# A graph network's edge kernel: the columns' list, the weights and the checks at other places, and two more groups by column copies

## The chip, the cores and the metric

The kernel runs on one core of a Trainium2 chip. The core has five engines, each with its own list of instructions that it works off in order: PE (matrix products; its weight loads are shown as a row of their own, PEld), DVE (vector operations), ACT (activation functions and copies), POOL (here: gathers of rows by index) and SP (which only issues transfers). PE writes to PSUM, a small memory that DVE and ACT read; everything else lies in SBUF, 128 partitions wide. Engines wait for one another through semaphores. Transfers from and to HBM are issued by SP, ACT or POOL and carried out by 16 DMA engines.

The metric is the device time of one launch in microseconds (us), the median of several executions. One further execution was profiled: its span runs from the first to the last instruction.

## The reference

One layer of message passing over 12,500 nodes with 64 features and 200,000 edges sorted by destination, then a residual and a normalisation:

```python
msg_in = concatenate([x[src], x[dst], edge_attr], axis=-1)     # 200000 x (64 + 64 + 32)
messages = relu(msg_in @ mW1 + mb1) @ mW2 + mb2                # hidden width 128, out 64
aggregated = segment_sum(messages, dst, 12500)
upd_in = concatenate([x, aggregated], axis=-1)
y = x + relu(upd_in @ uW1 + ub1) @ uW2 + ub2
out = (y - mean(y)) / sqrt(var(y) + 1e-5)                      # per node
```

All of it is in float32. The destinations are not uniform: low node numbers have more edges.

## The kernel before, in words

**Tables.** `x @ mW1[:64]` (for the source) and `x @ mW1[64:128] + mb1` (for the destination) are computed once per node. The first goes to a table `tab_a` in HBM, from which POOL gathers rows by source index; the second to `tab_b`, of which windows of 32 consecutive rows are read, because sorted edges have neighbouring destinations.

**Tiles and groups.** The edges form 1563 tiles of 128. Six tiles are a *group* `s` (261 groups, the steps of the main loop), twelve tiles a *super-group* `g`. For a group, `edge_part(s)` (line 401) multiplies, tile by tile, a stationary operand `l` (32 edge features and a 32-row selection of the destination, made by DVE in `select_rows`, L276) with `rhs` (edge weights and the window of `tab_b`) into the PSUM tile `pc` (L414). `node_part(s)` (422) adds the gathered rows by a product with the identity (L443) and notes the tile for DVE's relu (`positive`, L467). `collect(s)` (485) sums the hidden rows `h` by destination into PSUM (`sums`, L507) and counts them (`cnt`, L503).

**Copied groups.** For some groups, listed in `COPIED`, the last two of the six tiles are not gathered. Instead the 128 source columns of the transposed features (`xtop`, `xbot` in SBUF) are copied one by one into a tile `xc`, some by ACT (`singly`, L384) and some by DVE (`joined`, L392); each copy handles one column for two tiles, its address read from the list `col_a` by a register load (L360, one for eight copies). PE then multiplies `xc` with the first weights (L417). `PACE` holds pairs (first step, groups per step); `progress(s)` sums them, and a group is copied piece by piece so that it is ready three steps before its use. `col_a` is made in `columns_list()` (333): two loads from HBM into a tile of the pool tag `tb` (four buffers, shared with the chunks of the tables), then four DVE operations (L342).

**Updates.** Every few steps a block of up to 416 nodes is complete; `update`, `activated`, `residual`, `squares`, `statistics`, `deviation`, `norm` and `store` carry it through the second network to the output. The first update comes at step 46. For it the second layers are folded in advance in `weights()` (857): PE and DVE by turns (L860 to L873).

**Checks.** The kernel is written for destinations that fit its windows. `checks()` (875) tests that: the largest and the smallest offset in `drc` (two reductions over 1563 columns, L880 and L881), the order of the windows (L885), the size of the update blocks. The result is a flag, read at the very end (L1033); where it is set, a general loop follows that does not run here.

**Order of the work.** The order on each engine is written out by hand. Start-up (lines 741 to 827) makes `tab_a` in 13 chunks (`chunk_a`), each with copies by ACT and DVE into a `tb` buffer and a write by SP; between them stand loads, the first selections and the addresses of all windows (`offsets`). Then `columns_list()` is called, then the main loop (915). In a step `s` PE's order is: `node_part(s)`, `collect(s - 1)`, parts of updates, from step 11 on now and then a chunk of `tab_b`, `edge_part(s + 1)`, and what `rest(s)` (829) issues. `rest` loads in steps 1 to 7 what `drc` needs, issues at step 11 (`BS`) the loads of the second layers on ACT's queue and fills constants on DVE, and calls at step 13 `weights()` and `checks()`. Gathers on POOL are paced: most of them wait for a named matmul. After step 257 a tail written out by hand (992 to 1030) finishes the last groups and blocks.

## Time and profile before

| | us |
|---|---|
| median of 3 executions (lowest, highest) | 2132.93 (2130.94, 2138.86) |
| the profiled execution, its own time | 2131.12 |
| its span, first to last instruction | 2129.4 |
| busy PE / PEld | 1680.7 / 1272.8 |
| busy ACT | 1568.5 |
| busy POOL | 1250.2 |
| busy DVE | 1177.9 |

The mean granted clock of PE was 0.783 of full speed; it moves between 0.5 and 1 within the span. In the first 53 us the DMA engines are 80% busy, in the next 53 us 70%, later 20 to 30%. A row of the profile names the kernel's line, the engine, the operation, the tile written and those read, how often, the busy time and the mean length of one; behind the bar comes how long the engine was idle just before, and what ended that. "issue" means that nothing in the profile explains the wait.

### The profile page before, as it was taken

To read this page: it belongs to the slowest core of one execution; us is meant where nothing else is said; L and a number is where in the kernel's file an instruction comes from. 1 tells how busy PE (TensorE), PEld (TensorE's weight loads), DVE (VectorE), ACT (ScalarE), POOL (GpSimd) and SP (SyncE) were. 2 spreads that over 40 slices of the span, in tenths; PEclk is the share of its full clock that TensorE was granted. 3 is DMA by queue.
4 is the path that set the end of the run, shared out by engine and by line. 5 is a ranking of instruction groups with operands and counts; after the bars stand their busy time and mean duration, and the time that the engine had idled before them with its cause. 6 is when DMAs were issued, how large, how long until landed. Compare 5 with 4: busy or idle time off the path is not lost. (4 is left out here: it accounts for less than half of the span.)

```text
span 2129.4 us, 48279 instructions
## 1 busy us (share of the span) xinstructions
PE 1680.7 (79%) x10746; PEld 1272.8 (60%) x10746; DVE 1177.9 (55%) x8420; ACT 1568.5 (74%) x8066; POOL 1250.2 (59%) x1330
## 2 busy tenths in 40 slices
PE   3577877887787778777877887887888888888887
PEld 3465656665555556555555656665666666666666
DVE  5436565555555555565554555555555555555555
ACT  2296968759869687789686877777776868687773
POOL 6564665666666566665665555655566666666660
PEclk7677787787787777777887777877787788788889
DMA  8723333322222222223222322323232333333331
GB/s 204 192 77 92 89 95 89 96 85 73 80 75 79 75 75 82 76 79 84 77 82 78 89 80 81 89 83 92 85 85 81 92 87 92 88 93 88 90 88 53
DMA packets 207649, 190.05 MB, mean 89 GB/s; under 512 B 57814, under 2 KB 173998, under 8 KB 207358
## 3 DMA queue, kind: packets, MB, share of 16 engines
q1 hardware_dynamic: 163292, 100.05, 16.7%
q0 software_dynamic: 42272, 85.08, 14.5%
q10 hardware_dynamic: 1794, 1.80, 0.4%
q8 instruction: 90, 1.47, 0.3%
q14 instruction: 201, 1.64, 0.3%
HBM read 168.76 MB, written 18.02 MB: 88 GB/s over the span
## 5 line engine op out<-in xcount | busy, mean ns | idle before, releaser
L242 POOL DMA_INDIRECT xg<-tab_a,src_s x1273 | 1201.6, 944 | 807.5 <-issue 267.4
L384 ACT ACTIVATE xc<-xtop,xbot 128x1 f32 x7912 | 1499.0, 280 | 166.8 <-issue 136.7
L392 DVE TENSOR_TENSOR xc<-xtop,xbot 128x1 int32 x7576 | 634.0, 154 | 494.4 <-issue 479.0
L507 PE MATMUL sums<-band,h 128*128 128x96 f32 x3126 | 538.4, 326 | 155.4 <-issue 107.5
L507 PEld LDWEIGHTS sums<-band,h 128*128 128x128 f32 x3126 | 475.5, 232 | 185.3 <-issue 121.2
L443 PE MATMUL pc<-xg,band 128*128 128x256 f32 (+1 forms) x988 | 447.6, 582 | 27.8 <-issue 26.7
L414 PE MATMUL pc<-rhs,l 64*128 64x128 f32 x3126 | 370.6, 356 | 70.3 <-issue 60.6
L414 PEld LDWEIGHTS pc<-rhs,l 64*128 64x128 f32 x3126 | 293.3, 238 | 122.1 <-issue 94.2
L467 DVE TENSOR_SCALAR h<-pc 128x768 f32<-128x768 f32 x247 | 235.1, 952 | 175.7 <-remote 59.4
L443 PEld LDWEIGHTS pc<-xg,band 128*128 128x128 f32 x988 | 214.8, 240 | 141.1 <-issue 97.0
L276 DVE TENSOR_TENSOR l<-l,cps 128x768 f32<-128x768 int32 (+1 forms) x134 | 126.9, 947 | 132.7 <-PE pc L443 38.8
L503 PEld LDWEIGHTS <-one 128*1 128x1 bf16 x1563 | 57.0, 81 | 224.5 <-issue 219.9
L588 ACT ACTIVATE y<-cps 128x256 f32<-128x256 f32 (+1 forms) x36 | 13.7, 379 | 174.8 <-issue 106.2
L503 PE MATMUL cnt<-band,one 128*1 128x32 bf16 x1563 | 90.7, 180 | 55.3 <-issue 54.8
L571 ACT ACTIVATE hTu<-sums,ub_s 128x416 f32<-128x416 f32 (+1 forms) x36 | 21.6, 599 | 127.9 <-remote 47.4
L417 PE MATMUL pc<-band,xc 64*128 64x128 f32 x484 | 77.4, 313 | 8.5 <-issue 6.8
L679 PE MATMUL pb<-band,xtop 64*128 64x128 f32 x208 | 48.2, 396 | 44.8 <-DVE tb L687 29.4
L284 DVE TENSOR_TENSOR band<-cps,drc 128x384 f32<-128x384 f32 x131 | 71.5, 546 | 19.0 <-remote 16.1
L679 PEld LDWEIGHTS pb<-band,xtop 64*128 64x128 f32 x208 | 40.7, 286 | 53.0 <-DVE tb L687 31.2
L417 PEld LDWEIGHTS pc<-band,xc 64*128 64x128 f32 x484 | 63.9, 227 | 9.8 <-issue 9.7
L581 PE MATMUL cps<-u2c,hTu 128*128 128x64 f32 x284 | 54.0, 340 | 14.6 <-issue 14.0
L242 POOL DMA_INDIRECT xg<-in_x,src_s x48 | 47.6, 992 | 24.0 <-issue 12.8
(110 smaller groups left out, 646.1 us busy)
## 6 DMA issues: line engine op xcount, KB each, us to landing
l<-in_dst_row SPq DMA_DIRECT2D x262, 96.0 KB
l<-in_eT SPq DMA_DIRECT2D x262, 96.0 KB
xg<-tab_a,src_s POOLq DMA_INDIRECT x1273
rhs<-tab_b SPq DMA_DIRECT2D x361, 32.0 KB
tab_b<-tb SPq DMA_DIRECT2D x13, 512.0 KB
rhs<-tab_b SPq DMA_DIRECT2D x387, 16.0 KB
tab_a<-tb SPq DMA_DIRECT2D x12, 512.0 KB
out<-y SPq DMA_DIRECT2D x35, 128.0 KB
```

What stands on the lines that cost most here:

```text
L242: ins = nc.gpsimd.indirect_dma_start(out=a[:, i, :] if s < XG else a[:, i // 2, i % 2, :], out_offset=None, in_=A[:, :] if s >= XG else x[ ...
L276: nc.vector.tensor_tensor(l[r], l[r].bitcast(I32), node[r].unsqueeze(2).broadcast_to([r.stop - r.start, SUP // 2, P]), op=ALU.is_equal)
L284: nc.vector.tensor_tensor(s[:, :nt], slot.unsqueeze(1).broadcast_to([P, nt, WIN]), drc[:, g * SUP:g * SUP + nt].unsqueeze(2).broadcast_to( ...
L384: nc.scalar.activation(o[:, e:e + 1], top.bitcast(F32), AF.Identity, bias=bot.bitcast(F32))
L392: nc.vector.tensor_tensor(o[:, e:e + 1].bitcast(I32), top.bitcast(I32), bot.bitcast(I32), op=ALU.bitwise_or)
L414: done = nc.tensor.matmul(pc[:, b, k, :], L[g][q:q + 64, m, :], rhs[g % 2][q:q + 64, w, :], start=k == 0, stop=ends and not copied)
L417: done = nc.tensor.matmul(pc[:, b, k, :], xc[s][q:q + 64], w1a[q:q + 64], start=False, stop=ends)
L443: added = nc.tensor.matmul(pc[:, b, :m], ident, a[:, b, :m], start=False, stop=True)
L467: nc.vector.tensor_scalar(h, pc, 0.0, None, op0=ALU.max)
L503: nc.tensor.matmul(pn8[:, bass.ds(cs[i] - CBASE, 4 * WIN)].bitcast(F32), one, SB[g][:, k0 + i, :, 1], start=False, stop=ends and i == n - 1)
L507: made.append(nc.tensor.matmul(ps8[:, bass.ds(ws[i] - SBASE[u % 2], 4 * WIDE * WIN)].bitcast(F32), h[:, i % 2, i // 2, :], widened(g, k0 + i),
L679: nc.tensor.matmul(pb[:, h, i, :], (xbot if h else xtop)[64 * h:64 * h + 64, (c + HB * h + i) * P:(c + HB * h + i + 1) * P], w[64 * h:64 * ...
```

## The change

1. `columns_list()` is split. `columns_asked()` issues the two loads of the list in start-up behind the ninth chunk (k == 8) instead of after the last; `columns_list(cols)` makes `col_a` on DVE behind the twelfth chunk (k == 11).
2. The seven loads of the second layers, on ACT's queue, move from step 11 of the loop to start-up, one behind each of the chunks 2 to 8; the constants' fills on DVE move there too, behind chunk 1. `weights()` moves from step 13 to step 1.
3. `checks()` is cut in four. The part on windows and blocks, `nodes_checked()`, stays at step 13; the two large reductions, `largest()` and `smallest()`, and the flag, `flagged()`, go to the tail.
4. `PACE` changes: copies start at step 5 instead of 3, with 0.54 groups per step up to step 30, then 0.5, and from step 50 on 0.004 to 0.008 groups per step more than before. 123 groups instead of 121 are copied; the list of which ones shifts by a step over large stretches.

```diff
-PACE = ((3, 0.474), (50, 0.501), (130, 0.479), (170, 0.465), (261, 0))
+PACE = ((5, 0.54), (30, 0.5), (50, 0.505), (130, 0.487), (170, 0.473), (261, 0))
...
-        def columns_list():
+        def columns_asked():
...
+            return cols
+
+        def columns_list(cols):
+
+            for r in range(2):
+                n = min(P, NSUB - 1 - LEAD - r * P)
                 for b, base in enumerate((XBASE, YBASE)):
                     nc.vector.tensor_scalar(col_a[:n, r, :, b], cols[:n, r, b], 4.0, float(base), op0=ALU.mult, op1=ALU.add)
...
+        weight_loads = {2: (w2, mW2), 3: (u1a, uW1[D:2 * D, :]), 4: (b2c, mb2.rearrange("(f o) -> f o", o=1)),
+                        5: (uz[D:], uW1[0:D, :]), 6: (ux[ONE:ONE + 1], ub2.rearrange("(o f) -> o f", o=1)),
+                        7: (ub1_s, ub1.rearrange("(f o) -> f o", o=1)), 8: (u2, uW2)}
         for k, c in enumerate(range(0, NB, NCH)):
             copied = chunk_a(c)
...
+            if k == 1:
+                nc.vector.memset(uz[:D], 0.0)
...
+                nc.vector.tensor_copy(ux[D:], ident[D:, D:])
+            if k in weight_loads:
+                o, i = weight_loads[k]
+                nc.scalar.dma_start(o, i)
+            if k == 8:
+                cols = columns_asked()
+            if k == 11:
+                columns_list(cols)
...
-        columns_list()
         assert not first
...
             if s == BS:
                 nc.sync.dma_start(wa, wrow.rearrange("o (p c) -> (o p) c", c=NSUP))
                 nc.sync.dma_start(wb, wnext.rearrange("o (p c) -> (o p) c", c=NSUP))
-                nc.scalar.dma_start(w2, mW2)
...
-                nc.scalar.dma_start(u2, uW2)
+            elif s == 1:
+                weights()
             elif s == BS + 2:
-                weights()
-                checks()
+                nodes_checked()
...
+        def largest():
+
+            nc.vector.tensor_reduce(mm[:, 0:1], drc, AX.X, ALU.max)
+
+        def smallest():
+
+            nc.vector.tensor_reduce(mm[:, 1:2], drc[:, :NT - 1], AX.X, ALU.min)
+
+        def flagged():
+
+            r = E - (NT - 1) * P
+            nc.vector.tensor_tensor(mm[:r, 1:2], mm[:r, 1:2], drc[:r, NT - 1:], op=ALU.min)
+            nc.vector.tensor_scalar(mm[:, 0:1], mm[:, 0:1], float(WIN - 1), None, op0=ALU.is_gt)
+            nc.vector.tensor_scalar(mm[:, 1:2], mm[:, 1:2], 0.0, None, op0=ALU.is_lt)
+            nc.vector.tensor_reduce(mm[:, 3:4], mm[:, 0:3], AX.X, ALU.add)
+            pf = psum.tile([1, 1], F32, name="pf", tag="pc")
+            nc.tensor.matmul(pf, mm[:, 3:4], ones, start=True, stop=True)
             nc.vector.tensor_tensor(flag_i, pf, bad, op=ALU.add)
...
         close_sums(K - 2)
+        largest()
         residual(K - 3)
...
         norm(K - 3)
+        smallest()
         store(K - 3)
...
         update(K - 1)
+        flagged()
         activated(K - 1)
```

More of the change, by code (lines that the diff above doesn't have):

```diff
@@ L819, in gnn_kernel @@
                 counts(g)
+            if k == 1:
+                nc.vector.memset(uz[:D], 0.0)
+                nc.vector.memset(ux[:D], 0.0)
+                nc.vector.memset(eps, EPS)
+                nc.vector.memset(ones, 1.0)
+                nc.vector.tensor_copy(ux[D:], ident[D:, D:])
[6 more added lines that the diff above has]
+                columns_list(cols)
             if k > 3:
@@ L873, in weights, with nodes_checked @@
                 nc.vector.tensor_scalar(w, v, mean, None, op0=ALU.subtract)
-        def checks():
-            mm = work.tile([P, 4], F32, name="mm", bufs=1)
-            r = E - (NT - 1) * P
-            nc.vector.tensor_reduce(mm[:, 0:1], drc, AX.X, ALU.max)
-            nc.vector.tensor_reduce(mm[:, 1:2], drc[:, :NT - 1], AX.X, ALU.min)
-            nc.vector.tensor_tensor(mm[:r, 1:2], mm[:r, 1:2], drc[:r, NT - 1:], op=ALU.min)
+        mm = work.tile([P, 4], F32, name="mm", bufs=1)
+        bad = work.tile([1, 1], F32, name="bad", bufs=1)
+        def nodes_checked():
             back = work.tile([SUP, NSUP], F32, name="back", bufs=1)
@@ L887, in checks @@
             nc.vector.tensor_reduce(mm[:SUP, 2:3], back, AX.X, ALU.add)
-            nc.vector.tensor_scalar(mm[:, 0:1], mm[:, 0:1], float(WIN - 1), None, op0=ALU.is_gt)
-            nc.vector.tensor_scalar(mm[:, 1:2], mm[:, 1:2], 0.0, None, op0=ALU.is_lt)
-            nc.vector.tensor_reduce(mm[:, 3:4], mm[:, 0:3], AX.X, ALU.add)
-            pf = psum.tile([1, 1], F32, name="pf", tag="pc")
-            nc.tensor.matmul(pf, mm[:, 3:4], ones, start=True, stop=True)
             uf = work.tile([1, K + 1], F32, name="uf", bufs=1)
```

11 lines of the change are left out of this document (removed).

## The prediction

> **What bounds the kernel now.** I read the page first: busy times, the chain, the costliest groups.
>
> ```profile
> span 2129.4 us, 48279 instructions
> PE 1680.7 (79%) x10746; PEld 1272.8 (60%) x10746; DVE 1177.9 (55%) x8420; ACT 1568.5 (74%) x8066; POOL 1250.2 (59%) x1330
> ...
> L242 POOL DMA_INDIRECT xg<-tab_a,src_s x1273 | 1201.6, 944 | 807.5 <-issue 267.4 <-remote 193.4 <-PE pc L443 127.4
> L384 ACT ACTIVATE xc<-xtop,xbot 128x1 f32 x7912 | 1499.0, 280 | 166.8 <-issue 136.7
> L392 DVE TENSOR_TENSOR xc<-xtop,xbot 128x1 int32 x7576 | 634.0, 154 | 494.4 <-issue 479.0
> ...
> L417 PE MATMUL pc<-band,xc 64*128 64x128 f32 x484 | 77.4, 313 | 8.5 <-issue 6.8
> ```
>
> No engine is full. PE is the busiest, and the gathers on POOL are held back on purpose until chosen matmuls are done (their idle time ends at L443). ACT and DVE spend most of their time on column copies. So I asked for the waits of the whole run, and for the span of one line that runs in every step.
>
> ```profile
> PE sums L507 <- DVE h L467: 34.0, 20, 4.8
> ...
> DVE h L467 <- PE sums L507: 55.7, 29, 4.2
> ...
> PE sums L507 <- DVE xc L392: 12.5, 6, 3.4
> ```
>
> ```profile
> L507 PE MATMUL sums<-band,h x3126: 242/275/530, 78.0 to 2120.5; 128*128 128x96 f32 x196
> ```
>
> The loop runs from 78.0 to 2120.5 us, 261 steps, so 7.83 us a step. PE waits for DVE in it 20 + 6 times, 46.5 us in all; DVE waits for PE longer (55.7 us in one row alone). PE's order of work therefore sets the pace, and what stops PE early in the loop delays all that follows. The change is about such stops, so I then read step 13, where the weights are prepared and the checks made (rows of PE, then of DVE, in order of time: start, length, what, in brackets the idle time before).
>
> ```profile
> 183.40 0.49 PE L417 MATMUL pc<-band,xc 64*128 64x128 f32 x4
> 184.93 0.30 PE L860 MATMUL pw<-band,w 128*64 128x128 f32 x1 [1.04 <-DVE xc L392]
> 187.91 0.79 PE L864 MATMUL pw<-u1a,w2T 64*128 64x128 f32 x2 [2.69 <-DVE w2T L862]
> 189.09 0.58 PE L867 MATMUL pw<-u1a,b2c 64*1 64x128 f32 x2 [0.39 <-DVE w2u L865]
> 195.65 0.19 PE L892 MATMUL pf<-ones,mm 128*1 128x1 f32 x2 [5.97 <-DVE mm L890]
> 195.77 2.08 PE L443 MATMUL pc<-xg,band 128*128 128x256 f32 x4
> ```
>
> ```profile
> 187.58 0.28 DVE L862 COPY w2T<-pw 64x128 f32<-64x128 f32 x1 [1.53 <-remote]
> ...
> 191.12 1.77 DVE L880 TENSOR_REDUCE mm<-drc 128x1 f32<-128x1563 f32 x1
> ...
> 194.69 0.28 DVE L885 TENSOR_TENSOR back<-wb,wa 12x131 f32<-12x131 int32 x1
> ```
>
> From 183.89 to 195.77 PE does next to nothing: it goes back and forth with DVE over the weights, then waits 5.97 us for DVE's checks, because the small matmul L892 stands in PE's order ahead of the gathered rows' sum (L443).
>
> **The change, part by part.** All terms are against this execution's own time, 2131.1 us (span 2129.4); it stands 1.8 us under the median of the runs shown and near the lowest.
>
> Step 13 empties. The weights' three matmuls and the checks' matmul leave it; what stays (L885 and its followers, on DVE alone) has no PE instruction behind it. PE goes from L417 to L443: 195.77 - 183.89 = **-11.9 us**. Bounds: -11.9, and -5.9 if the next steps make half of it up (a rival below).
>
> The clock after it. These windows give busy time by engine, then the granted clock (PEclk).
>
> ```profile
> 190.00:196.00 6.00, 0.35 (x3) 0.32 (x4) 5.69 (x19) 6.00 (x34) 0.00 (x0) 0.50 0.04 12
> 196.00:201.00 5.00, 5.00 (x24) 3.94 (x26) 3.02 (x26) 5.00 (x28) 0.94 (x1) 0.50 0.05 13
> 208.00:214.00 6.00, 4.99 (x49) 4.02 (x46) 4.82 (x35) 6.00 (x34) 3.26 (x4) 1.00 0.39 114
> ```
>
> PE comes out of the stall at half clock and works 5.00 us at it. At full clock, as at 208, the same work takes 2.5 us. As other stops halve the clock too, I take **-2 us**, bounds -2.5 and 0. The Trainium skill ("TensorE: Matmul & The Clock Gate", Part 1: The HAM clock gate) says that an idle window of about 3.4 us halves the clock and a busy one of that length frees it. By that rule the loss would be one window at half speed, an estimate of 1.7 us, and the sum 0.3 us higher; the trace shows the half clock for longer, over both windows quoted.
>
> The weight loads leave ACT's order at step 11.
>
> ```profile
> 166.25 0.33 ACTq L841 DMA_DIRECT2D w<-in_mW  x1
> ...
> 176.88 0.44 ACTq L852 DMA_DIRECT2D u<-in_uW  x1
> 178.65 1.59 ACT L384 ACTIVATE xc<-xtop,xbot 128x1 f32 x8 [16.72 <-DMA u<-in_uW]
> ```
>
> ACT loses 16.72 us there: the load of ux's row (L850) waits for DVE's fills of ux (L845, L848), which stand behind a table chunk. But no group waited: PE's L417 at 183.40 found its columns ready. I count **0**, bounds -3 (two or three copies late by a step) and 0.
>
> The weights' matmuls come at step 1 instead. The price is the chain itself: between 1.67 us (0.30 + 0.79 + 0.58, PE's own work) and 5.8 us (183.89 to 189.67, as at step 13, where DVE was late by other work). I take **+3.0 us**, nearer to 1.67, since DVE's copy at step 13 first sat idle for 1.53 us and PE has a wait of its own at step 1. Behind it in PE's order stands node_part(2), and POOL's paced gathers wait for that.
>
> The columns' list leaves the end of start-up. SP, PE and DVE there:
>
> ```profile
> 77.39 1.91 SPq L339 DMA_DIRECT2D cols<-in_src_row  x2
> 80.54 0.78 SPq L321 DMA_DIRECT2D rhs<-tab_b  x1
> ...
> 84.19 1.65 PE L414 MATMUL pc<-rhs,l 64*128 64x128 f32 x12 [4.31 <-issue]
> ...
> 99.41 1.01 PE L433 MATMUL pc<-band,sums_s 64*128 64x128 f32 x5 [4.01 <-ACT sums_s L330]
> ...
> 82.31 0.36 DVE L342 TENSOR_SCALAR col_a<-cols 128x128 int32<-128x128 int32 x2 [10.84 <-DMA cols<-in_src_row]
> ```
>
> SP issues the list's two loads for 1.91 us before the table rows (L321) that PE's L414 at 84.19 reads. They now stand ahead of the ninth chunk, where SP waits anyway. PE's 4.31 us wait shortens by **-1.9 us**, bounds -4.3 and 0. DVE's 10.84 us wait is no gain of its own: the next thing DVE needs, the destination rows, comes from SP too.
>
> Start-up takes in all of this: seven loads (128 KB of matrices), 252 KB of list, and one of the four buffers "tb" for three chunks.
>
> ```profile
> 46.00:62.00 16.00, 4.16 (x32) 3.57 (x32) 12.63 (x29) 1.44 (x2) 11.73 (x11) 0.50 1.10 269
> ...
> 62.33 0.58 ACT L689 COPY tb<-pb 128x512 f32<-128x512 f32 x1 [14.63 <-remote]
> ```
>
> ACT's issues (0.33 to 0.6 us each) fall into waits like that of 14.63 us, and the list's load stands behind it, when the queues have drained. I take **+0.5 us**, bounds 0 and 14.6 (one more such wait for a buffer).
>
> The copies: 123 groups instead of 121, by PACE 1.2 of the two added groups by step 50; 128 more copies on ACT and 128 on DVE, four gathers less. Copies start at step 5, not 3. ACT's price is 1499.0 / 7912 = 0.189 us, so 24.3 us if ACT set the pace; DVE's comes from these two runs of eight.
>
> ```profile
> 206.49 0.65 DVE L392 TENSOR_TENSOR xc<-xtop,xbot 128x1 int32 x8 [1.64 <-issue]
> 207.95 0.67 DVE L392 TENSOR_TENSOR xc<-xtop,xbot 128x1 int32 x8 [0.82 <-issue]
> ```
>
> Eight take 207.95 - 206.49 = 1.46 us, 0.183 each, so 23.4 us if DVE did. Four gathers are 4 x (944 + 210) ns = 4.6 us (210 ns: 267.4 / 1273 of issue), if POOL did. PE gets 8 more L417 matmuls, 1.3 us at most. PE waited for DVE 26 times in 261 steps, a tenth; a tenth of 23.4 is **+2.3 us**, bounds -4.6 and +24.3.
>
> The tail takes the two large reductions and the flag.
>
> ```profile
> 2111.03 0.42 DVE L597 TENSOR_REDUCE ss<-y 128x4 f32<-128x256 f32 x1 [1.41 <-ACT y L588]
> ...
> 2116.15 0.62 DVE L453 TENSOR_TENSOR h<-xg,pc 128x256 f32<-128x256 f32 x2 [2.59 <-PE pc L414]
> ```
>
> At 1.77 us (L880; L881 reads one column less), the first falls into the wait of 1.41 us, the second into that of 2.59 us. That leaves **+0.4 us**; uncovered, both cost 3.5 us.
>
> Sum: -11.9 - 2 + 0 + 3.0 - 1.9 + 0.5 + 2.3 + 0.4 = -9.6, so **2121.5 us**, 0.5% under the median of 2132.93. About 0.5% is also what a measurement of this kernel can tell from no change (2122.3 and 2143.6 us), so the forecast lies just on the faster side.
>
> **Rivals.** *Given back.* During PE's stall ACT and DVE worked on. PE then did three steps quickly:
>
> ```profile
> 198.02 2.88 PE L507 MATMUL sums<-band,h 128*128 128x96 f32 x12
> ...
> 215.60 1.25 PE L507 MATMUL sums<-band,h 128*128 128x96 f32 x9
> ```
>
> 17.6 us instead of 3 x 7.83 = 23.5 us: 5.9 us were made up, and removing the stall removes that too. Against it: PE had another long stop soon after. Result 2121.5 + 5.9 = **2127.4**.
>
> *Slower: DVE's copies set the pace.* In steps 5 to 29 a rate of 0.54 means 0.54 x 64 = 35 copies a step, 6.3 us of DVE at 0.183, beside DVE's other work. If that fills the step, every added copy counts: 23.4 instead of 2.3, so 2121.5 + 21.1 = **2142.6**. It decides once PE's wait for L467 (34.0 us) appears in most steps. Against it: DVE waits for PE more than PE for DVE.
>
> *More goes.* In step 3 PE issues one matmul at a time from 90.4 us on and then waits until 99.41:
>
> ```profile
> 89.73 0.71 PE L414 MATMUL pc<-rhs,l 64*128 64x128 f32 x7
> ...
> 95.04 0.36 PE L414 MATMUL pc<-rhs,l 64*128 64x128 f32 x1 [1.15 <-issue]
> ```
>  If this comes from the late list and SP's late loads, up to 8 us more fall away, or the weights' chain hides in it: 2121.5 - 8 = **2113.5**. Against it: other such stretches occur all through the loop ("issue").
>
> *Start-up fills.* The list and the weights, 380 KB, go at 269 GB/s through engines that are full from 46 to 62 us (share 1.10): 1.4 us. If a chunk misses its buffer, one more wait of 14.63 us comes: about **2136**. The Trainium skill ("DMA: Bandwidth & Descriptors", Issuing engines are not separate DMA queues) speaks for this: loads issued by ACT run on the same 16 engines and interleave with SP's.
>
> **How the numbers follow.** Forecast 0.45 (own range 2115 to 2127), given back 0.20, DVE's copies 0.15, more goes 0.14, start-up 0.06. Faster: some 0.28 of the forecast's, 0.14 of "more goes", 0.03 of "given back": 0.45. Slower: half of DVE's case and 0.06 from the copies' upper bound on ACT: 0.14. The rest, 0.41, is same. The range leaves out the outer part of DVE's case and the far end of "more goes": 2109 to 2138.
>
> **What would show it.** Right: PE goes from L417 to L443 in step 13 without a gap of microseconds; ACT's 16.72 us wait is gone; the first L414 of step 1 starts some 2 us earlier; the span shrinks by about what step 20 starts earlier. Wrong: step 17 or so starts at nearly the same time (given back); PE's waits for L467 or L392 grow over 46.5 us (DVE); the loop's first L507 comes later than 78.0.

## The result and the profile after

The changed kernel took 2127.31 us (median of 11 executions, 2121.67 to 2132.47) beside 2132.95 us for the kernel before on the same chip (11 executions, 2127.61 to 2138.86). The ratio is 0.9976, 95% interval 0.9966 to 0.9986: 0.24% faster where 0.54% was forecast. It lies in the predicted range, just above the forecast's own part of it (2115 to 2127), and inside the 0.5% that the prediction called "same". The sign was right, the size less than half. That 2127.31 is the figure of the rival "Given back" (2127.4) is chance: of the 5.9 us that this rival names, the traces show 1.5 (below).

The page of the kernel after, its waits, and the row of `sums` with the bounds of its times (lines moved by six: L390 is the former L384, L398 the former L392, L513 the former L507, L473 the former L467):

```profile
span 2124.8 us, 48559 instructions
PE 1676.5 (79%) x10754; PEld 1267.3 (60%) x10754; DVE 1187.5 (56%) x8547; ACT 1590.6 (75%) x8194; POOL 1246.8 (59%) x1326
...
L390 ACT ACTIVATE xc<-xtop,xbot 128x1 f32 x8040 | 1520.3, 280 | 120.8 <-issue 101.4
```

```profile
DVE h L473 <- PE sums L513: 57.2, 37, 4.9
...
PE sums L513 <- DVE h L473: 43.9, 27, 6.7
...
PE sums L513 <- DVE xc L398: 16.6, 7, 3.5
```

```profile
L513 PE MATMUL sums<-band,h x3126: 242/275/529, 85.2 to 2115.4; 128*128 128x96 f32 x196
```

The loop now starts at 85.2 us, 7.2 later than before (78.0), and the last product of this kind comes 5.1 us earlier (2120.5 before). So the loop itself became some 12 us shorter, and start-up took most of that back. PE's waits for DVE grew from 46.5 to 60.5 us (43.9 + 16.6).

Step 13, the place of the forecast's largest term, in the timeline of PE after:

```profile
181.11 1.04 PE L420 MATMUL pc<-rhs,l 64*128 64x128 f32 x12 [3.78 <-issue]
181.88 0.53 PE L423 MATMUL pc<-band,xc 64*128 64x128 f32 x4
182.35 2.07 PE L449 MATMUL pc<-xg,band 128*128 128x256 f32 x4
...
184.60 2.88 PE L513 MATMUL sums<-band,h 128*128 128x96 f32 x12
...
190.75 1.58 PE L513 MATMUL sums<-band,h 128*128 128x96 f32 x12
...
198.77 1.64 PE L420 MATMUL pc<-rhs,l 64*128 64x128 f32 x11 [5.35 <-DVE h L473]
```

PE goes from the copied columns' product (L423) to the gathered rows' (L449) without a gap, as forecast. The reader should see the last row too: a step later PE stands 5.35 us for DVE's `h`, which in the kernel before was ready in time, presumably because the stall had let DVE work ahead.

Start-up after, ACT's copies of chunks and the first PE work that follows them:

```profile
65.24 0.58 ACT L695 COPY tb<-pb 128x512 f32<-128x512 f32 x1 [9.93 <-DVE lists L743]
...
73.94 0.59 ACT L695 COPY tb<-pb 128x512 f32<-128x512 f32 x1 [5.33 <-DMA tab_a<-tb]
78.50 0.37 ACT L695 COPY tb<-pb 128x256 f32<-128x256 f32 x1 [3.97 <-DMA tab_a<-tb]
```

```profile
78.92 1.72 PE L420 MATMUL pc<-rhs,l 64*128 64x128 f32 x12 [8.31 <-ACT tb L695]
...
87.45 0.94 PE L420 MATMUL pc<-rhs,l 64*128 64x128 f32 x12 [0.31 <-issue]
88.31 0.30 PE L870 MATMUL pw<-band,w 128*64 128x128 f32 x1
...
92.12 1.65 PE L439 MATMUL pc<-band,sums_s 64*128 64x128 f32 x12
```

The last two chunks wait 5.33 and 3.97 us for the writes of earlier chunks, since a buffer is missing; PE waits 8.31 us behind them. Before, the last chunk's copy was made at 72.01 us. From 72 to 77 us PE does nothing while the DMA engines are full (columns: time, busy PE, PEld, DVE, ACT, POOL, then clock, DMA share, GB/s):

```profile
72.00:77.00 5.00, 0.00 (x0) 0.00 (x0) 1.23 (x5) 0.59 (x1) 1.10 (x2) 0.50 1.12 311
```

The weights' chain stands from the end of L420 (88.39) to L439 (92.12).

Both traces, by the start of the first `sums` product of a step (us; the tail's end is the span):

| stretch | before | after | difference gained (-) or lost | forecast |
|---|---|---|---|---|
| start to step 0 | 78.0 | 85.2 | +7.2 | +0.5 |
| step 0 to 12 (list, weights) | 103.1 | 99.4 | -3.7 | -1.9 + 3.0 |
| step 12 to 13 (stall) | 16.9 | 6.2 | -10.7 | -11.9 |
| step 13 to 19 (clock, DVE) | 44.6 | 46.1 | +1.5 | -2 |
| step 19 to 250 (copies) | 1824.1 | 1820.5 | -3.6 | +2.3 |
| step 250 to the end | 62.7 | 67.4 | +4.7 | +0.4 |
| sum | 2129.4 | 2124.8 | -4.6 | -9.6 |

Single steps before step 20 jump by some 3 us between the two traces without a wait that is named ("issue"), so each of the first rows is uncertain by about that. Later the difference wanders more: it is -10.1 us at step 60 and -2.0 at step 65. The -3.6 of the stretch from step 19 to 250 therefore lies within the scatter of two single executions.

### The profile page after: what moved, and what is told of

It reads as the page before. It is cut to its first block, busy times and chain, and to the rows that moved or that the text cites. A ratio compares the mean times of both kernels' runs of the same rounds, so it can differ in the third digit from the quotient of the medians.

```text
span 2124.8 us, 48559 instructions
## 1 busy us (share of the span) xinstructions
PE 1676.5 (79%) x10754; PEld 1267.3 (60%) x10754; DVE 1187.5 (56%) x8547; ACT 1590.6 (75%) x8194; POOL 1246.8 (59%) x1326
## 5 line engine op out<-in xcount | busy, mean ns | idle before, releaser
L390 ACT ACTIVATE xc<-xtop,xbot 128x1 f32 x8040 | 1520.3, 280 | 120.8 <-issue 101.4
L398 DVE TENSOR_TENSOR xc<-xtop,xbot 128x1 int32 x7704 | 644.4, 153 | 514.4 <-issue 496.7
L513 PE MATMUL sums<-band,h 128*128 128x96 f32 x3126 | 530.2, 322 | 161.4 <-issue 99.5
L513 PEld LDWEIGHTS sums<-band,h 128*128 128x128 f32 x3126 | 466.5, 229 | 195.4 <-issue 118.1
L449 PE MATMUL pc<-xg,band 128*128 128x384 f32 (+1 forms) x988 | 452.3, 585 | 36.2 <-issue 31.1
L420 PE MATMUL pc<-rhs,l 64*128 64x128 f32 x3126 | 372.7, 355 | 86.3 <-issue 56.8
L420 PEld LDWEIGHTS pc<-rhs,l 64*128 64x128 f32 x3126 | 294.1, 237 | 135.2 <-issue 88.0
L473 DVE TENSOR_SCALAR h<-pc 128x768 f32<-128x768 f32 x247 | 235.1, 952 | 146.0 <-PE sums L513 57.2
L449 PEld LDWEIGHTS pc<-xg,band 128*128 128x128 f32 x988 | 217.6, 243 | 154.3 <-issue 110.0
L594 ACT ACTIVATE y<-cps 128x256 f32<-128x256 f32 (+1 forms) x36 | 13.7, 380 | 178.3 <-issue 64.1
L509 PE MATMUL cnt<-band,one 128*1 128x32 bf16 x1563 | 89.9, 180 | 43.9 <-issue 42.5
L423 PE MATMUL pc<-band,xc 64*128 64x128 f32 x492 | 78.1, 313 | 11.2 <-issue 11.1
L423 PEld LDWEIGHTS pc<-band,xc 64*128 64x128 f32 x492 | 64.6, 226 | 9.8 <-issue 9.8
L685 PEld LDWEIGHTS pb<-band,xtop 64*128 64x128 f32 x208 | 40.1, 283 | 47.5 <-issue 25.0
```

Of the source, the lines that this page charges most:

```text
L390: nc.scalar.activation(o[:, e:e + 1], top.bitcast(F32), AF.Identity, bias=bot.bitcast(F32))
L398: nc.vector.tensor_tensor(o[:, e:e + 1].bitcast(I32), top.bitcast(I32), bot.bitcast(I32), op=ALU.bitwise_or)
L420: done = nc.tensor.matmul(pc[:, b, k, :], L[g][q:q + 64, m, :], rhs[g % 2][q:q + 64, w, :], start=k == 0, stop=ends and not copied)
L423: done = nc.tensor.matmul(pc[:, b, k, :], xc[s][q:q + 64], w1a[q:q + 64], start=False, stop=ends)
L449: added = nc.tensor.matmul(pc[:, b, :m], ident, a[:, b, :m], start=False, stop=True)
L473: nc.vector.tensor_scalar(h, pc, 0.0, None, op0=ALU.max)
```

## The experiments

The experiments ran on five chips, and with the result's chip these are of two kinds. On the chip of the result and on that of the runs e13 to e15 the kernel before takes about 2131 us at a mean granted clock of 0.78. On the chips of all other runs it takes about 1683 us at 0.88. So run e7 took the profile of the kernel before there. First the page's busy times and the waits of PE of e7, then the waits of PE of the kernel before on the result's chip:

```profile
PE 1386.4 (83%) x10746; PEld 1083.3 (65%) x10746; DVE 1162.3 (69%) x8420; ACT 1539.4 (92%) x8066; POOL 1253.6 (75%) x1330
```

```profile
PE sums L507 <- DVE h L467: 133.7, 84, 4.6
PE cnt L501 <- DVE xw L528: 61.5, 24, 5.2
```

```profile
PE sums L507 <- issue: 107.5, 147, 3.6
PE pc L414 <- issue: 60.6, 103, 4.3
PE cnt L503 <- issue: 54.8, 75, 1.5
```

And the windows of 500 to 900 us, e7 first, then the kernel before on the result's chip:

```profile
500.00:900.00 400.00, 325.91 (x2433) 253.59 (x2431) 277.62 (x2161) 394.08 (x2111) 302.23 (x320) 0.87 0.37 99
```

```profile
500.00:900.00 400.00, 311.06 (x1933) 231.77 (x1931) 218.78 (x1694) 317.14 (x1671) 241.32 (x256) 0.78 0.27 76
```

On the second kind ACT is busy for 394 of 400 us: its column copies set the pace (for how much of the run, e8 below shows). On the first it is busy for 317, and PE has over 200 us of waits behind which the profile shows nothing; on the second kind they are gone. What causes them stays open; each chip of the experiments was used on one occasion only, so whether chip or occasion makes the kind is open too. It matters for all that follows: an edit of the copies has another price on either kind.

**The parts one by one** (second kind of chip, each against the kernel before). The edits are the four parts of the change, each alone.

> The kernel before with one part alone: the checks cut in four, two reductions and the flag in the tail; weights and list stay where they were. Theory A (the gain of step 13 is real and stays, start-up took most of it back in the full change): start-up is untouched (first L507 within 1.5 us of 78.0), in step 13 PE no longer waits 5.97 us for the checks, about 6 of the 11.9 us go, and 4 to 6 us of that are left at step 19: 2127 to 2129, ratio 0.997 to 0.998. Theory B (given back): the steps 14 to 17 make it up in any case, at step 19 less than 2 us are left: 2131 to 2133, ratio 0.999 to 1.000. Theory C (the tail takes it): step 250 starts 5 us or more earlier, but the end does not: over 2131, with the tail 4 us longer than before.

> The kernel before with one part alone: the seven loads of the second layers and the constants in start-up, the weights' matmuls at step 1; checks and list stay. Theory A1 (the list costs start-up its 7 us): the first L507 stays within 2 us of 78.0; step 13 loses about 5.8 us (its stretch up to 189.67), step 1 gains up to 3: 2129 to 2132, ratio 0.998 to 1.000. Theory A2 (the loads cost start-up its time, since their bytes are in the full stretch from 30 to 62 us): the first L507 comes 4 to 7 us later, ratio 0.999 to 1.003. Theory B (given back): step 13's gain is gone by step 19, and the price of step 1 is left: 2134 to 2137.

> The kernel before with one part alone: the columns' list asked for behind the ninth chunk and made behind the twelfth. Theory A1 (the list, with one of the four buffers of the chunks and its 252 KB in the full stretch, costs start-up its time): the first L507 4 to 8 us later than 78.0, and since nothing gains, 2135 to 2139, ratio 1.001 to 1.003. Theory A2 (the loads cost it): the first L507 within 2 us of 78.0 and the forecast's gain of 1.9 us at SP: 2129 to 2133, ratio 0.998 to 1.000. Theory D (chance: start-up scatters by several us from run to run): neither this nor the part with the loads shows the 7 us, or both show it in part.

> The kernel before with one part alone: the new list of copied groups (123 for 121). The forecast's term: +2.3 us, between -4.6 and +24.3: 2133 to 2137, ratio 1.000 to 1.002. Theory E (the copies take some of the gain: the steps from 5 to 30 lose at the rate of 0.54): steps 5 to 30 take 3 us or more longer than before, ratio 1.002 or more. Theory F (fewer gathers are worth more than the copies cost, and this part carries the gain): steps 20 to 250 take 4 us or more less, ratio 0.998 or less.

> The changed kernel as it is, timed beside the kernel before on the chip on which the four single parts are compared. There the kernel before took 1682.6 us, and ACT was busy for 92% of the span. If the parts add up (checks -4.5, weights +3.4, list 0.1, copies +38.8 us): +37.8 us, ratio 1.0225. If the copies' price depends on the state of the chip alone and this chip is again one where the kernel before takes about 2133: ratio 0.9976 as before. If the parts hide one another (a late start gives ACT time to work ahead): less than the sum, ratio 1.010 to 1.020.

> The changed kernel with the old list of copied groups: list, weights and checks moved, nothing else. Sum of the three parts on the chip where the kernel before took 1682.6 us: -4.5 + 3.4 + 0.1 = -1.0 us, ratio 0.999 to 1.000. Rival (list and loads meet in start-up, and together cost what neither does alone): the first L507 5 us or more later than with either alone, ratio 1.002 or more. Rival (step 13 is empty only when both its parts are gone, and the 11.9 us of the forecast show then): step 13 gains 10 us or more against the kernel before, ratio 0.995 or less.

> The kernel before, unchanged, for its profile on the chip of the experiments: which engine is full there. If ACT sets the pace on it, ACT is busy for over 95% of the steps from 20 to 250 and waits for nothing there; if PE does, PE's waits for DVE stay as small as in the profile before (46.5 us) and ACT waits for its next group.

| run | part | us | before | ratio | 95% interval |
|---|---|---|---|---|---|
| e1 | checks cut in four | 1677.60 | 1682.64 | 0.9973 | 0.9959 to 0.9987 |
| e2 | weights early | 1685.08 | 1682.64 | 1.0020 | 1.0005 to 1.0034 |
| e3 | list early | 1681.96 | 1682.64 | 1.0001 | 0.9989 to 1.0013 |
| e4 | new list of groups | 1721.08 | 1682.64 | 1.0232 | 1.0212 to 1.0251 |
| e5 | all four | 1722.07 | 1683.89 | 1.0225 | 1.0202 to 1.0247 |
| e6 | all but the new list | 1682.97 | 1683.89 | 0.9996 | 0.9984 to 1.0007 |
| e17 | e6 on a further chip | 1681.43 | 1682.93 | 1.0001 | 0.9987 to 1.0015 |

The parts add up: the ratios of e1 to e4 give 1.0226, measured 1.0225; those of e1 to e3 give 0.9994, measured 0.9996 and 1.0001. There the changed kernel is 2.25% slower, by the new list of groups alone; the three moves together are worth nothing. Where this comes about, by the start of the first `sums` product of a step, in us against e7:

| step | e7 | e1 checks | e2 weights | e3 list | e6 three | e4 groups |
|---|---|---|---|---|---|---|
| 0 | 61.2 | +0.8 | +3.7 | +3.1 | +7.5 | -1.1 |
| 2 | 76.6 | +1.2 | +8.5 | -1.2 | +7.0 | +0.4 |
| 12 | 139.5 | +4.0 | +7.9 | -1.4 | +7.4 | -3.0 |
| 13 | 155.2 | -2.4 | +4.6 | -1.2 | -4.0 | -0.2 |
| 20 | 200.0 | -1.0 | +4.6 | -1.4 | -0.4 | +2.9 |
| 250 | 1618.9 | -2.1 | +7.9 | -1.5 | +0.4 | +32.3 |
| 260 | 1669.5 | -3.1 | +7.4 | -2.1 | +2.8 | +38.9 |

Start-up's +7.5 in e6 is the +7.2 of the result, on another kind of chip: it is no accident of one run. Loads and list each give about half, so of e1's to e3's readings the expected A1 and A2 each hold in part. But the list's +3.1 is gone by step 2: what SP no longer does before the table rows gives it back (from +3.1 to -1.1 at step 1). The weights' loss is not; it grows to +8.5, and step 13 returns only 3.3 of it.

These are single executions. Five traces with the start-up of the kernel before (e1, e4, e7, e8, e18) start step 0 at 58.8 to 62.0 us, so a difference of 2 us there says little. e17, the same kernel as e6, has +6.3 at step 0 and step 2. Behind step 20 the ratios say more than the table: e2's execution took 3.1 us more than the median of its runs, e6's 3.3 more, and e7's 3.1 less than the median on its chip. By the medians the weights' part costs 2.4 us in all. e6's 4.2 us between steps 258 and 260 (-1.4 to +2.8) are not in e17.

e6 empties step 13 by 11.4 us (+7.4 to -4.0), as forecast, and gives 3.6 of it back by step 20. Step 13 with the checks alone away (e1) and the row that takes the stall's place in e6, PE's timeline:

```profile
147.84 0.30 PE L860 MATMUL pw<-band,w 128*64 128x128 f32 x1 [1.55 <-DVE h L467]
149.20 0.49 PE L864 MATMUL pw<-u1a,w2T 64*128 64x128 f32 x2 [1.06 <-DVE w2T L862]
150.07 0.58 PE L867 MATMUL pw<-u1a,b2c 64*1 64x128 f32 x2 [0.38 <-DVE w2u L865]
150.58 2.07 PE L443 MATMUL pc<-xg,band 128*128 128x256 f32 x4
```

```profile
157.73 1.66 PE L420 MATMUL pc<-rhs,l 64*128 64x128 f32 x12 [3.86 <-DVE h L473]
```

Without the checks behind them the weights hold PE for 150.58 - 147.84 = 2.7 us at step 13. They had been cheap where they stood.

**Start-up: loads, buffer, places.** Starting from e6, e9 issues the seven loads behind the last chunk, e10 loads the list into an idle tile, e11 does both; e12 adds seven loads of four bytes to the kernel before.

```diff
 e9, e11 (the new lines stand behind the loop over the chunks)
-            if k in weight_loads:
-                o, i = weight_loads[k]
-                nc.scalar.dma_start(o, i)
+        for o, i in weight_loads.values():
+            nc.scalar.dma_start(o, i)
 e10, e11
-            cols = work.tile([P, 2, 2, P], I32, name="cols", tag="tb", bufs=4)
+            cols = hT.bitcast(I32).rearrange("p (k b e) -> p k b e", k=2, b=2)
 e12
+        spare = work.tile([1, 8], F32, name="spare", bufs=1)
...
+            if 2 <= k <= 8:
+                nc.scalar.dma_start(spare[:, k - 2:k - 1], mb2[k:k + 1].rearrange("(o f) -> o f", o=1))
```

> The changed kernel with the old list of copied groups (as in the run 'oldpace', whose first L507 came 7.5 us late), and the seven loads of the second layers issued together behind the last chunk in place of one behind each of the chunks 2 to 8. Theory 'loads in between hold up SP' (SP's transfers wait there for the landing of loads that ACT issued): SP's wait for ub_s is gone, the first L507 comes 3 to 5 us earlier than in 'oldpace', less what ACT spends on seven issues (7 x 0.45 = 3.2 us) where its next copy waits for them: ratio 0.997 to 0.998. Theory 'the list alone costs it' (one of four buffers): the first L507 stays 6 us or more late, ratio 0.999 to 1.000.

> The changed kernel with the old list of copied groups, and the columns' list loaded into the tile hTu, which is idle in start-up, in place of one of the four buffers tb. Theory 'buffer': ACT's last two copies of chunks no longer wait 5.4 and 3.4 us for tab_a's writes, the first L507 3 to 4 us earlier than in 'oldpace': ratio 0.997 to 0.998. Theory 'bytes' (252 KB of list in full DMA engines): no buffer is short, the list's bytes still cost their 1 us or so, and the first L507 is less than 1.5 us earlier: ratio 0.999 to 1.000.

> Both of these edits in one kernel. If the two causes are separate and are all of start-up's loss: first L507 within 2 us of the kernel before (61.2 us on the chip of the run 'before'), and what step 13 gains stays: ratio 0.995 to 0.997, faster than both kernels. If they meet in one resource (the DMA engines), the sum is less than the two gains: ratio 0.997 to 0.999.

> The kernel before, and seven loads of four bytes each into a spare tile on ACT's queue behind the chunks 2 to 8, nothing else; their data are not used. Theory 'places' (each transfer of SP waits for an earlier transfer, and ACT's loads take places in that order, whatever their size): the first L507 comes 2.5 us or more late, as with the real loads alone (+3.7), and the whole is 1.0015 to 1.003 times the kernel before. Theory 'bytes' (128 KB of weights in full engines): within 1 us of the kernel before, ratio 0.999 to 1.001.

| run | ratio | 95% interval | step 0 | step 2 | step 20 |
|---|---|---|---|---|---|
| e9 loads late | 0.9994 | 0.9978 to 1.0010 | +9.9 | +7.1 | -0.1 |
| e10 list in hTu | 0.9999 | 0.9983 to 1.0016 | +3.3 | +8.1 | +1.3 |
| e11 both | 0.9974 | 0.9960 to 0.9989 | +3.7 | +7.1 | +1.2 |
| e12 tiny loads | 1.0005 | 0.9990 to 1.0020 | +1.2 | +1.2 | +2.5 |

(The steps are of one profiled execution each, against e7. e11's took 1682.66 us, 3.8 more than the median of its runs, so its ratio tells more than its steps.) e10 gives step 0 back 4.2 us against e6 and 3.0 against e17, so the missing buffer is shown as a cause of about half of the loss where the loads are moved too. ACT's last two copies of chunks, in e6 and then in e10:

```profile
57.79 0.59 ACT L695 COPY tb<-pb 128x512 f32<-128x512 f32 x1 [5.41 <-DMA tab_a<-tb]
61.78 0.37 ACT L695 COPY tb<-pb 128x256 f32<-128x256 f32 x1 [3.40 <-DMA tab_a<-tb]
```

```profile
53.56 0.59 ACT L695 COPY tb<-pb 128x512 f32<-128x512 f32 x1 [2.11 <-DVE xbot L676]
58.24 0.37 ACT L695 COPY tb<-pb 128x256 f32<-128x256 f32 x1 [4.10 <-DMA tab_a<-tb]
```

The last copy comes 3.5 us earlier, though it still waits for a write; in e7 it came at 55.08. Without the loads the list in an idle tile is worth less: e3 starts step 0 at 64.3 us, and e16 (below), which has it so, at 63.4.

The gain of e9 or e10 alone does not show in the whole time: both were expected at 0.997 to 0.998 if their cause was the right one, and neither reached it. Of the four only e11, with both edits, is faster than the kernel before, at the 0.997 to 0.999 that it was to have if the two meet in one resource. Step 2 stays 6 to 8.5 us late in all kernels that fold the weights at step 1 (e17 has +6.3, e2 +8.5), wherever loads and list go. The loss only changes its place. In e2 SP stands for a load of ACT's; in e9 it stands far longer, and in e11 PE waits for an ACT copy behind the seven issues (waits of SP in e2, then in e9, then PE's row in e11):

```profile
SPq L660 <- DMA ub_s<-in_ub: 4.9, 1, 4.9
```

```profile
SPq L669 <- DMA w<-in_mW: 10.4, 1, 10.4
```

```profile
59.55 1.65 PE L439 MATMUL pc<-band,sums_s 64*128 64x128 f32 x12 [4.61 <-ACT sums_s L330]
```

Nothing in the kernel makes a load of `xtop` or `xbot` depend on one of the weights. The compiled program does: SP's and ACT's transfers use eight completion counters, and each first waits for the one that held its counter (here two neighbouring transfers of SP, in the kernel before and then in e6, where ACT's first load has taken a place ahead of them; a counter's name is DMAHW with a number):

```
13 L691 DMA tab_a<-tb 128x8x128 [waits DMAHW3_49,DVE_49]
14 L636 DMA wh<-in_whalf 64x48 [waits DMAHW4_49]
...
13 L697 DMA tab_a<-tb 128x8x128 [waits DMAHW4_49,DVE_49]
14 L642 DMA wh<-in_whalf 64x48 [waits DMAHW5_49]
```

Further on, the profile of e6 has what comes of it: SP waits 5.7 us at a load of `xtop` (L666) for the load of `ub_s`.

e12 tests what such a place costs by itself. SP's waits appear (3.1 and 1.0 us for the spare tile; a wait for `xbot` like the 3.8 us here stands in e1 too, with 3.5), but step 0 comes only 1.2 us later, which e1 shows nearly as large (0.8) without any load, and the ratio's interval holds 1. So the places make the waits; that they cost "2.5 us or more" by themselves is not borne out, though the scatter of step 0 does not exclude some 2 us. What the real loads add, bytes or the later landing, was not separated.

Of the 8 us at step 2 the chain on PE is 3 to 4: 76.94 - 73.56 = 3.4 in e2, 92.12 - 88.39 = 3.7 in the kernel after. In e2 the table rows come later than in e3, which has the list early and the weights late (the first L414 of step 1, then the fold and L433 in e2; L420 and L439 in e3):

```profile
71.97 1.65 PE L414 MATMUL pc<-rhs,l 64*128 64x128 f32 x12 [5.12 <-issue]
73.56 0.42 PE L861 MATMUL pw<-band,w 128*64 128x128 f32 x1
...
76.94 1.65 PE L433 MATMUL pc<-band,sums_s 64*128 64x128 f32 x12
```

```profile
68.18 1.41 PE L420 MATMUL pc<-rhs,l 64*128 64x128 f32 x12 [1.95 <-issue]
69.32 1.55 PE L439 MATMUL pc<-band,sums_s 64*128 64x128 f32 x12
```

That is 3.8 us at L414 (71.97 - 68.18; both the list and the loads are in it) and 3.4 for the chain, 7.6 between the two L433/L439. The rest of e2's +8.5 against e3's -1.2 comes after them, with PE's products of that step taking longer; it was not tested by itself.

**The copies.** e8 has 117 groups; e14 and e18 have 123, all rates 0.008 higher, from step 3 as before; e15 has 121 from step 5.

```diff
-PACE = ((3, 0.474), (50, 0.501), (130, 0.479), (170, 0.465), (261, 0))
+PACE = ((3, 0.458), (50, 0.485), (130, 0.463), (170, 0.449), (261, 0))     e8
+PACE = ((3, 0.482), (50, 0.509), (130, 0.487), (170, 0.473), (261, 0))     e14, e18
+PACE = ((5, 0.495), (50, 0.501), (130, 0.479), (170, 0.465), (261, 0))     e15
```

> The kernel before with all rates of the list of copied groups lowered by 0.016: 117 groups in place of 121, 264 copies less on ACT, 248 less on DVE, eight gathers more. Theory 'ACT sets the pace': 264 x 0.185 us = 49 us less work on ACT; since eight gathers (10 us on POOL at 1.25 us each) come back, POOL sets the pace next and the gain ends at 5 to 20 us: ratio 0.988 to 0.997. Theory 'POOL sets the pace': 10 us more, ratio 1.004 to 1.007. Theory 'PE sets it' (the forecast's reading): 16 matmuls less, within 3 us, ratio 0.998 to 1.002.

> The kernel before with 123 copied groups, all rates raised by 0.008, start at step 3 as before: 128 copies more on ACT, 128 on DVE, four gathers less. If the number alone makes the new list dear (+38.8 us): ratio 1.020 or more. If ACT is full and each copy costs its length: 128 x 0.189 = 24.2 us, ratio 1.012 to 1.016. If the late start at step 5 costs the most: ratio 1.000 to 1.008.

> The kernel before with 121 copied groups as before, but copies starting at step 5 in place of 3, at 0.495 groups a step up to step 50 in place of 0.474, and the old rates behind it. If ACT is full, the two steps in which it has no copies to make (0.95 groups, 62 copies, 11.6 us) cannot be won back: +10 to +16 us, ratio 1.006 to 1.010. If only the number counts: ratio 0.999 to 1.001.

> The kernel before with 123 copied groups, all rates raised by 0.008, once more. On a chip where the kernel before takes about 2131 us: 0.997 again. On a chip where it takes about 1683 us: if ACT is full and each copy costs its length, 24.2 us, ratio 1.012 to 1.016; the rest of the new list's 38.8 us is then the start at step 5. If the late start is all of it: 1.000 to 1.003.

| run | kind of chip | us | before | ratio | 95% interval |
|---|---|---|---|---|---|
| e8, 117 groups | second | 1683.83 | 1683.89 | 0.9997 | 0.9982 to 1.0012 |
| e18, 123 groups | second | 1707.66 | 1682.93 | 1.0151 | 1.0129 to 1.0173 |
| e14, 123 groups | first | 2123.41 | 2131.27 | 0.9969 | 0.9958 to 0.9980 |
| e15, from step 5 | first | 2136.28 | 2131.27 | 1.0028 | 1.0014 to 1.0042 |

Where ACT is full, 128 copies cost 24.7 us (1707.66 - 1682.93), which is ACT's 128 x 0.189 = 24.2; the loss grows over the whole run (+5 at step 50, +12 at 100, +22 at 200). The rest of the new list's 38.4 us is 13.7. By the traces some 6 of it stand by step 256 (e4 +33.0, e18 +27.2), and some 7 come in the tail (below). The first part may be the two steps without copies at the start (62 copies, 11.6 us of ACT that cannot be won back); e15, made to show this, fell on the first kind, so there it is only argued. The step times agree with it in sign: in e4 steps 4 and 5 start 4.6 and 7.3 us early, with no copies to make, and step 30 11.1 us late, where e18 is 5.1 late.

Fewer copies (e8) gained nothing on the whole, though "ACT sets the pace" had put the gain at 5 to 20 us. Its ratio falls into the range that was named for PE at the pace, but its steps tell another story: e8 is 25.3 us ahead of e7 at step 170 and 1.1 behind at step 250. From 1200 us on PE waits for gathered rows, and in e7 nowhere (e8's waits of PE, 1200 to 1620 us):

```profile
PE pc L443 <- DMA xg<-tab_a,src_s: 29.5, 38, 2.2
```

So fewer copies do pay as long as ACT is what holds the steps up, and in the last third the gathers, eight more of them, take the gain back.

Where ACT has room (first kind), 123 groups make the kernel faster by 7.9 us (e14), and e15 is slower by 5.0; none of the readings written down for these two runs had foreseen either. Their traces don't tie the times to the copies. Of e14's 8.0 us against the kernel before on the result's chip, 5.8 stand at step 20, and 3.6 of these at step 1, before any copy is made; e15 is 0.3 us early at step 30 and 1.9 late at step 250.

In the tail, e4 and e5 lose 6 us between steps 256 and 258 (+33.0 to +38.9 and +34.0 to +40.1); e1 and e18 do not. It is the new list's, not the checks'. Its last copied group is 256, not 257, but that this is the reason was not tested. The kernel after, which loses 7.2 us there, shows what happens. PE's rows, and the window behind them:

```profile
2095.43 0.64 PE L420 MATMUL pc<-rhs,l 64*128 64x128 f32 x4 [0.98 <-DMA rhs<-tab_b]
2097.24 0.33 PE L509 MATMUL cnt<-band,one 128*1 128x32 bf16 x6 [1.17 <-issue]
```

```profile
2097.00:2107.00 10.00, 9.77 (x49) 8.62 (x49) 5.49 (x9) 0.68 (x2) 0.00 (x0) 0.50 0.18 50
```

PE waits for a window of `tab_b`, then works 10 us at half clock; the kernel before had 0.83 there.

**Versions that leave the weights alone.** e13 has the checks cut in four and the list early in hTu; e16 adds the 123 groups from step 3.

> The kernel before with the checks cut in four and the columns' list early, loaded into hTu; weights, their loads and the list of copied groups as before. If start-up's loss has the two causes named (loads in between, one buffer taken) and both are absent here: first L507 at 60 to 63 us, step 1 about 4 us earlier than in the kernel before (the list out of SP's way), step 13 as in the run 'checks' (-5 to -6 us), ratio 0.994 to 0.996, faster than both kernels. If the list's early place gains nothing once ACT's copies set the pace: ratio 0.997 to 0.998, the same as the checks alone.

> The kernel of the run 'best' (checks cut in four, columns' list early into hTu, weights as before) with the list of the run 'count' (123 copied groups from step 3). On a chip where the kernel before takes about 2131 us, the two gains add: -5.6 and -7.9 us, ratio 0.993 to 0.995, faster than the changed kernel (0.9976). If they hide one another there: 0.996 to 0.998. On a chip where it takes about 1683 us, the copies' price (128 x 0.189 = 24.2 us, as far as ACT is full) outweighs the rest: 1.007 to 1.013.

> The changed kernel with the old list of copied groups once more, for the chip that this set gets. On a chip where the kernel before takes about 2131 us: if the changed kernel's gain there (0.24%) comes from list, weights and checks, and the new list of groups is worth nothing (two more groups -7.9, late start +4.3 us): ratio 0.996 to 0.999. If the copies carry it: 0.999 to 1.002. On a chip where it takes about 1683 us: 0.9996 again.

e13 took 2125.65 us beside 2131.27, ratio 0.9976 (0.9965 to 0.9988), on the first kind: the whole of the changed kernel's gain, without the weights' move or the new groups. Its step 0 starts 1.3 us late, step 1 4.1 early, step 13 11.2 early, against the kernel before on the result's chip. The 4.1 can't be put down to the list, since e14 has 3.6 there with the list at its old place; in e16, which has the list early and the weights late on the second kind, step 1 is 1.3 us late against e7. e13's ratio is the 0.997 to 0.998 of the lower expectation, but the reason given for it, ACT's copies at the pace, does not hold on this kind. e16 fell on the second kind, 1702.26 beside 1682.93, ratio 1.0118 (1.0096 to 1.0140): dearer by the copies, as expected there. The sum of both gains on the first kind was not measured, and neither was e6 on it.

No version was found that beats both kernels by more than the interval on both kinds; of those tried, only the 123 groups were timed on both. The checks' cut is in what is faster on either: 0.9973 alone on the second (e1), and 0.9976 together with the list on the first (e13), where it was not timed alone.

## Why the prediction was right and wrong

**Right:** the place and size of the main term. Step 13 emptied by 10.7 us on the result's chip and 11.4 in e6 (forecast 11.9); PE passes from L423 to L449 without a gap. The chain of the weights on PE, taken at 3.0, was 3.4 to 3.7. ACT's wait of 16.72 us is gone (its timeline after; 95 copies without a break), and, as the term of 0 said, no gain of its own appears beside the stall's:

```profile
167.52 17.71 ACT L390 ACTIVATE xc<-xtop,xbot 128x1 f32 x95 [0.39 <-issue]
```

**Wrong, the failing step:** "Start-up takes in all of this ... I take +0.5 us". It was +7.2, within its bounds of 0 and 14.6 but far from the value taken. The reasoning was that ACT's issues fall into its waits and that the list comes when the queues have drained. The list stands for about half of it and the loads for the other half (+3.1 and +3.7 alone, +7.5 and +6.3 with both). The buffer is what the list cost beside the loads: the chunks' copies waited 5.33 and 3.97 us for one, and e10 got 3.0 to 4.2 us back by sparing it. Of the loads' share, what the traces show is SP standing behind ACT's transfers, in the kernel after too (SP's waits there):

```profile
SPq L260 <- DMA ux<-in_ub: 7.0, 1, 7.0
```

The rival "Start-up fills" named the right mechanism (a chunk misses its buffer); it got 0.06, and its price of 14.63 us was twice too high. The Trainium skill ("DMA: Bandwidth & Descriptors", Issuing engines are not separate DMA queues) says that transfers of all issuers interleave on the same engines; no run here separates that from engines that are full in any case, and SP's waits for ACT's loads (4.9 us in e2, 7.0 in the kernel after) go beyond it.

**Half wrong: list and weights.** The list's -1.9 was too small for the stretch: -4.2 from step 0 to 1 in e3 (+3.1 to -1.1), near the bound of -4.3. But 3.1 of this only make up the list's own loss in start-up; with both counted it is -1.1 at step 1 in e3 and +1.3 in e16, so a gain by the list is not shown. The weights' +3.0 counted only the chain; with their loads they put step 2 back by 8.5 us (e2; 2.4 of the whole time by the medians), and the stall they left at step 13 was 2.7 us once the checks behind it were gone. On the result's chip the stretch from step 0 to 12 still gained 3.7 us where +1.1 was forecast; after e14's 3.6 us at step 1 this may be scatter.

**Wrong in sign: the clock.** "I take -2 us" became +1.5: PE's next wait is for DVE's `h` (5.35 us at 198.77), and the clock fell there again. So the rival "Given back" holds for a part, 1.5 us on the result's chip and 3.6 in e6, not for 5.9. That a busy stretch frees the clock, which the Trainium skill ("TensorE: Matmul & The Clock Gate", Part 1: The HAM clock gate) says, the trace after shows again, at 0.52 and then 0.83 in these two windows:

```profile
182.00:187.00 5.00, 5.00 (x28) 3.95 (x25) 2.38 (x17) 4.39 (x25) 3.38 (x4) 0.52 0.48 140
187.00:193.00 6.00, 6.00 (x49) 4.62 (x50) 5.14 (x36) 6.00 (x34) 3.67 (x5) 0.83 0.38 107
```

**Copies and tail.** +2.3 was forecast for two more groups. On the result's kind of chip e14 measures -7.9 for the number and e15 +5.0 for the late start, about -3 together, near the -3.6 seen from step 19 to 250. The agreement proves little: between these steps e14's trace gains nothing and e15's loses 3.8. The term had taken a tenth of what the copies cost DVE, with -4.6 for four gathers less as its lower bound; e14's -7.9 is beyond that, though its interval reaches from -4.3 to -9.0, and the runs don't show how four gathers less can save that much. The rival with DVE at the pace did not happen: PE's waits for DVE reached 60.5 us, over the 46.5 named as its sign, but the steps became shorter. On the second kind the term came to 38.4 us, above its upper bound of 24.3: the bound took ACT's price for 128 copies, and left out some 6 us that the new list adds before the tail (the late start, as argued above) and some 7 in it. The tail's +0.4 for the checks holds (e1 loses nothing behind step 250, -2.1 to -2.9 by the span); the +4.7 seen comes with the new list, as e4 and e5 show.

**Signs.** Of the signs named for being right, three came true: no gap at step 13, no wait of 16.72 us on ACT, and a span that shrinks (4.6 us) by about what step 20 starts earlier (4.8). The first product of step 1 did not come some 2 us earlier: it starts at 87.45, where it was 84.19. Of the signs named for being wrong, two appeared: PE's waits for DVE over 46.5 us, and the loop's start later than 78.0.

Summed up, the forecast erred by +6.7 in start-up, -4.8 up to step 12, +1.2 at the stall, +3.5 behind it, -5.9 in the copies and +4.3 in the tail: +5.0, from -9.6 to -4.6. Errors of both signs hid one another; only the stall's term was right by itself.

## What to carry to other kernels

A stage that is full has no idle places: when work moves into a start-up whose DMA engines and buffers are in use, price the buffer it takes and the transfers that now stand in line behind it, not only its bytes. Before a chain is moved, ask what it costs where it stands once its neighbour has gone: the weights held PE for 2.7 us at step 13, and folded at step 1 they put step 2 back by 6 to 8.5. A single execution can differ from the median by more than the term that is looked for, so such a term needs several, or another cause for trusting it. A rate tuned to an engine with room is worth less than nothing where that engine is full, so profile on the chip where it is to run.

## What was not expected of the hardware

The same program ran in about 2131 us on one kind of chip and about 1683 on the other. The mean granted clock was 0.78 and 0.88; beyond that PE had 107.5 + 60.6 + 54.8 = 222.9 us of waits before three of its lines that the profile explains by nothing, and 8.1 us (5.9 + 2.0 + 0.2) on the other kind (e7). ACT's column copies (280 and 282 ns) and POOL's gathers (944 and 946 ns) last as long on both, so it is not these engines that are slower. The order of engines by load changes with the kind, and the sign of an edit: 0.9969 and 1.0151 for the same 123 groups.

The clock stayed at half for 10 us of the tail in which PE was busy for 9.77 (the window from 2097 to 2107 us above). The Trainium skill ("TensorE: Matmul & The Clock Gate", Part 1: The HAM clock gate) gives about 3.4 us of activity as enough to free it; here it was not, and the runs don't show why.
